# Output products of a graph layer, moved from the end of its edge loop into the loop

## The chip, the cores and the metric

The kernel runs on one core of a Trainium2 chip. The time is that of the device for one execution, in microseconds (us); the time before is the median of three executions. One more execution was taken by the hardware profiler, and all durations of single instructions come from that one.

In the profile, PE is the matrix engine (TensorE) and PEld its loading of weights, DVE the vector engine, ACT the scalar engine, POOL the GpSimd engine, SP the engine that issues most DMAs. L803 is line 803 of the kernel.

## The reference

Four graph layers follow one another over 1024 nodes with 512 features and 17408 edges. Each layer normalizes its input, applies a relu and adds its result to x. The edges are sorted by their receiving node `dst`.

```python
h = jnp.maximum(_layernorm(x, axis=-1), 0.0)
x = x + _L0_gnn_ref(h, edge_index, L0_gnn_weight, L0_gnn_bias)
h = jnp.maximum(_layernorm(x, axis=-1), 0.0)
x = x + _L1_gnn_ref(h, edge_attr_4, edge_attr_8, edge_index, ...)
h = jnp.maximum(_layernorm(x, axis=-1), 0.0)
x = x + _L2_gnn_ref(h, ...)
h = jnp.maximum(_layernorm(x, axis=-1), 0.0)
x = x + _L3_gnn_ref(h, src, dst, edge_type_8, edge_weight, ...)
```

The change touches the end of the second of them, L1 (block 1 in the kernel's numbering, which counts from 0):

```python
x0, x1 = _lin_irreps(x0, x1, W_up0, W_up1)
h = edge_feats
for W in (W_mlp1, W_mlp2, W_mlp3):
    h = SILU_2MOM * jax.nn.silu(h @ W / jnp.sqrt(jnp.float32(W.shape[0])))
tpw = h @ W_mlp4 / jnp.sqrt(jnp.float32(W_mlp4.shape[0]))
w1, w2, w3, w4 = jnp.split(tpw, 4, axis=-1)
s0 = x0[sender]
s1 = x1[sender]
p1 = w1 * s0 * y0
p2 = (w2 * s0)[:, :, None] * y1[:, None, :]
p3 = w3[:, :, None] * s1 * y0[:, None, :]
p4 = w4 * jnp.einsum('eum,em->eu', s1, y1) / SQRT3
m0 = jnp.concatenate([p1, p4], axis=-1)
m1 = jnp.concatenate([p2, p3], axis=1)
msg0 = jax.ops.segment_sum(m0, receiver, num_segments=num_nodes)
msg1 = jax.ops.segment_sum(m1, receiver, num_segments=num_nodes)
o0, o1 = _lin_irreps(msg0, msg1, W_out0, W_out1)
out = jnp.concatenate([o0, o1.reshape(num_nodes, 3 * MUL)], axis=-1)
return out / AVG_NUM_NEIGHBORS
```

So for every edge a message of 8 blocks of 128 features is made and summed at the edge's receiver; the sums of a node are then multiplied with two output matrices. These last two products, with the addition to x, are called the output products below. The layer after it, L2 (block 2), starts with the normalization and relu of the new x.

## The kernel before, in words

The nodes are cut into NB = 8 tiles of 128, the edges into NG = 68 groups of 256 (two tiles of 128 edges, G = 2). `stack(True)` is the arm of the kernel that runs for these inputs; in it a group's receivers lie in a window of W = 32 nodes, whose first node `base(g)` is read from memory into a register of DVE.

*Block 1's loop* (from line 870) runs over the groups. For group g it prepares the message of the next group and sums that of its own:

- `mixed(g + 1)`: four records on PE (L819, tile pw), the edge network's last product, from hidden values that SP loads (hq, L576).
- `message(g + 1)`: POOL gathers the senders' rows (L290, tile s), ACT makes six scaled copies (L836, dot), DVE five operations (L837 to L841) that write the message msg. The order of the operations on DVE, in the text, is: two products with pw, two additions of dot, one product with pw.
- `weighted(g + 1)`: POOL writes the receivers' one-hot rows, weighted (L859, yo).
- the sums of group g: 12 matmuls, 24 records on PE (L885, tile pg), into a bank of PSUM.
- `acc[:, :, base(g) : base(g) + W] += pg` on DVE (L888). acc holds the sums of all nodes, 8 blocks x 1024 nodes. Its place comes from a register, so nothing in the program says which nodes it touches.

From group 8 on, every fourth group also loads weights of block 2 or subtracts two of them on POOL (L765).

*Output products.* `out1(n)` multiplies node tile n of acc with the output matrices: 8 matmuls of 128 columns, 16 records on PE (L803, tile po), then two DVE operations that add the scaled result to x (L804, L806). At its end it calls `normed(n, "l2")`, the normalization and relu: DVE L208 and L209 (mean and variance), ACT L211 (root), DVE L217 and L219, ACT L227, which writes `h2[n]` (tile hl in the profile).

`settled(n)` is the number of the last group whose window can reach tile n: 11, 19, 28, 36, 45, 53, 62 for tiles 0 to 6. An input for which that doesn't hold takes the other arm. With EARLY = 2, `out1(0)` stands in the loop's group 66 and `out1(1)` in group 67. There the operations on DVE are kept in the written order by `pinned(DVE)`.

*After the loop*, `lagged(...)` (line 988) runs three stages over the tiles with a lag: `out1(n)` for the tiles not done yet, two tiles later the transposition of `h2` (`turned2`, PE L241, ACT L244), and one tile later still, for every second tile, the pair product `dense1` / `seven`: seven products of half size on PE (L955, 28 records) with DVE, ACT and POOL operations between them that end in the terms of block 2's propagation (L275).

*Order.* The program is written as one stream. A planner lays out each engine's queue at compile time: an instruction is put in the queue in the order of the text, unless it is not expected to be ready and a later one is. `pinned(...)` fixes the order of the instructions of an engine that are written in it, `issue_after(i)` puts instructions behind i on their engine. On the chip each engine works its queue in order and waits on semaphores.

*PSUM*: `bank(...)` gives one of four banks (pg, po, the transpositions, the pair products), `bank2(...)` one of two pairs of banks (pw). The normalized tiles `h` have four buffers, their small statistics two.

Of the kernel before, what the change touches and what calls it, by code (L numbers as in the profile page):

```python
# [23 lines left out]
NB = N // P  # L24
# [13 lines left out]
NG = ET // G  # L38
# [5 lines left out]
def settled(n):  # L44

    return (17 * (n + 1) + 1) // 2 + 2
# [3 lines left out]
def gnn_stack(ctx, tc, a, out, xtab, htabs, hidtab):  # L50
# [174 lines left out]
    def norm_relu(h, xn, name):  # L225
        rs, nm = stats(xn, name)
        rectified.append(nc.scalar.activation(h, xn, AF.Relu, bias=nm, scale=rs).ins)  # L227
# [4 lines left out]
    def normed(n, name):  # L232

        h = work.tile([P, D], F32, tag="h", name=f"h{name}_{n}", bufs=4)
        norm_relu(h, x[:, n, :], f"{name}_{n}")
        return h
# [26 lines left out]
    def lagged(*stages):  # L263

        for n in range(NB + max(lag for _, lag in stages)):
            for stage, lag in stages:
                if 0 <= n - lag < NB:
                    stage(n - lag)
# [118 lines left out]
    def stack(fast):  # L387
# [403 lines left out]
        EARLY = 2  # L791
        h2 = {}
# [3 lines left out]
        def out1(n):  # L796
            po = bank(f"po_{n}")
            ns = slice(n * P, (n + 1) * P)
            for c in range(KC):
                w = w_out0 if c == 0 else w_out1  # L800
                bl = (0, 1) if c == 0 else (1 + c, 4 + c)
                for k, b in enumerate(bl):
                    nc.tensor.matmul(po[:, c * P : (c + 1) * P], acc[:, b, ns], w[:, k, :], start=(k == 0), stop=(k == 1))  # L803
            nc.vector.scalar_tensor_tensor(x[:, n, :MUL], po[:, :MUL], scale, x[:, n, :MUL], op0=ALU.mult, op1=ALU.add)  # L804
            xm = x[:, n, MUL:].rearrange("p (u m) -> p m u", m=3)
            nc.vector.scalar_tensor_tensor(xm, po[:, MUL:].rearrange("p (m u) -> p m u", m=3), scale, xm, op0=ALU.mult, op1=ALU.add)  # L806
            h2[n] = normed(n, "l2")

        with tc.tile_pool(name=f"l1e{fast}", bufs=2 if fast else 1, reuse_waits="tile") as l1e:

            def mixed(g):

                q = g * G // 8
                if q not in hq:
                    fetch(q)
                pw = bank2(f"pw_{g}")
                for k in range(G):
                    t = g * G + k
                    nc.tensor.matmul(pw[:, k, :], hq[q][:, (t % 4) * P : (t % 4 + 1) * P], w_mlp4[:, t // 4 % 2, :],  # L819
                                     start=True, stop=True)  # L820
                return pw

            def message(g, pw):

                s = l1e.tile([P, G, D], F32, tag="s", name=f"s_{g}", bufs=3 if fast else 1)
                for k in range(G):
                    gather(s[:, k, :], xtab, src_i, g * G + k)
                w = pw.rearrange("p k (j u) -> p k j u", u=MUL)
                s0 = s[:, :, :MUL]
                s1 = s[:, :, MUL:].rearrange("p k (m u) -> p k m u", m=3)  # L830

                msg = l1e.tile([P, G, 6, MUL], F32, tag="msg", name=f"msg_{g}")
                dot = l1e.tile([P, G, 3, MUL], F32, tag="dot", name=f"dot_{g}", bufs=2 if fast else 1)
                for k in range(G):
                    for m in range(3):
                        nc.scalar.activation(dot[:, k, m, :], s1[:, k, m, :], AF.Copy, scale=ea[:, g * G + k, 1 + m : 2 + m])  # L836
                nc.vector.tensor_mul(msg[:, :, 0:2, :], w[:, :, 0:2, :], s0.unsqueeze(2).to_broadcast([P, G, 2, MUL]))  # L837
                nc.vector.tensor_mul(msg[:, :, 2:5, :], s1, w[:, :, 2:3, :].to_broadcast([P, G, 3, MUL]))  # L838
                nc.vector.tensor_add(dot[:, :, 0, :], dot[:, :, 0, :], dot[:, :, 1, :])
                nc.vector.tensor_add(dot[:, :, 0, :], dot[:, :, 0, :], dot[:, :, 2, :])  # L840
                nc.vector.tensor_mul(msg[:, :, 5, :], dot[:, :, 0, :], w[:, :, 3, :])  # L841
                return msg


            def blocks(msg, rhs):

                yield msg[:, 0, :], rhs(0, 1), 0, 1
                yield msg[:, 5, :], rhs(4, 1), 1, 1
                yield msg[:, 1, :], rhs(1, 3), 2, 3
                for m in range(3):  # L850
                    yield msg[:, 2 + m, :], rhs(0, 1), 5 + m, 1

            if fast:
                def weighted(g):
                    yo = l1e.tile([P, G, NY, W], F32, tag="yo", name=f"yo_{g}")
                    ts = slice(g * G, (g + 1) * G)
                    for k in range(G):
                        t = g * G + k
                        nc.gpsimd.tensor_mul(yo[:, k], ohw[:, t, :].unsqueeze(1).to_broadcast([P, NY, W]),  # L859
                                             ea[:, t, :].unsqueeze(2).to_broadcast([P, NY, W]))  # L860
                    return yo

                ahead = [weighted(0), weighted(1)]
                with pinned(PE, ACT):
                    fill(2)
                    pw = mixed(0)
                    fill(6)
                    nxt = message(0, pw), ahead.pop(0)
                    fill(3 * (NQ - NOW))
                for g in range(NG):  # L870
                    msg, yo = nxt
                    if g + 1 < NG:
                        nxt = message(g + 1, mixed(g + 1)), ahead.pop(0) if ahead else weighted(g + 1)
                    if g == 8:
                        blocks1 = load_l2()
                    if g >= 8 and g % 4 == 0:

                        with tc.issue_after(fetched[-1]):
                            next(blocks1, None)
                    ps = bank(f"pg_{g}")[:, : 8 * W].rearrange("p (b w) -> p b w", w=W)  # L880
                    prods = [list(blocks(msg[:, k], lambda y, n, k=k: yo[:, k, y : y + n, :])) for k in range(G)]
                    for i in range(len(prods[0])):
                        for k in range(G):
                            lhsT, rhs, b, n = prods[k][i]
                            nc.tensor.matmul(ps[:, b : b + n, :], lhsT, rhs, start=(k == 0), stop=(k == G - 1))  # L885
                    with pinned(DVE) if g >= NG - EARLY else nullcontext():
                        part = acc[:, :, bass.ds(base(g), W)]
                        nc.vector.tensor_add(part, part, ps)  # L888

                        if g >= NG - EARLY:  # L890
                            out1(g - NG + EARLY)
            else:
                for _ in load_l2():
                    pass
                for g in range(NG):
                    msg = message(g, mixed(g))
                    first = g == 0
                    for j in range(2):
                        for y, bl in ((0, ((0, 0), (2, 5), (3, 6), (4, 7))), (1, ((1, 2),)), (2, ((1, 3),)), (3, ((1, 4),)), (4, ((5, 1),))):
                            yo = l1e.tile([P, G, 512], F32, tag="yo", name=f"yo_{g}_{j}_{y}")  # L900
                            for k in range(G):
                                t = g * G + k
                                nc.vector.tensor_scalar(yo[:, k, :], iota[:, j * 512 : (j + 1) * 512], dst_f[:, t : t + 1],
                                                        ea[:, t, y : y + 1], op0=ALU.is_equal, op1=ALU.mult)
                            for c, b in bl:
                                ps = bank(f"pg_{g}_{j}_{b}")
                                for k in range(G):
                                    nc.tensor.matmul(ps, msg[:, k, c, :], yo[:, k, :], start=(k == 0), stop=(k == G - 1))
                                part = acc[:, b, j * 512 : (j + 1) * 512]
                                if first:  # L910
                                    nc.vector.tensor_copy(part, ps)
                                else:
                                    nc.vector.tensor_add(part, part, ps)
# [3 lines left out]
        with tc.tile_pool(name=f"l2{fast}", bufs=1) as l2:  # L917
# [67 lines left out]
                    for i in (n - 1, n):  # L985
                        nc.gpsimd.tensor_add(y[:, i, :], y[:, i, :], b1)

            lagged((lambda n: n in h2 or out1(n), 0), (turned2, 2), (dense1, 3))

            if fast:  # L990
                parts = l1.tile([P, 3, NB, D], BF16, tag="acc", name="parts2", bufs=1)
# [73 lines left out]
        with tc.tile_pool(name=f"l3{fast}", bufs=1, reuse_waits="tile") as l3:  # L1065
# [34 lines left out]
            for l in range(2):  # L1100
# [5 lines left out]
                with tc.tile_pool(name=f"l3e{l}{fast}", bufs=3 if fast else 1, reuse_waits="tile") as l3e:  # L1106
# [24 lines left out]
                    if fast:  # L1131
# [10 lines left out]
                        for g in range(NG):  # L1142
# [8 lines left out]
                            n = {0: 3, 1: 4, 2: 5, 4: 6, 6: 7}.get(g)  # L1151
# [109 lines left out]
```

## Time and profile before

| | |
|---|---|
| median of 3 executions | 1225.16 us (1224.23 to 1227.38) |
| profiled execution, its own time | 1221.29 us |
| its span, first to last instruction | 1219.5 us |
| mean granted clock of PE | 0.994 |
| PE busy in 340 to 380 us (inside the loop) | 40.00 of 40.00 us |
| DVE busy in 340 to 380 us | 28.78 of 40.00 us |
| ACT, POOL busy in 340 to 380 us | 17.87, 26.38 of 40.00 us |
| first pg of the loop, last pg | 178.6 us, 480.6 us |
| po of tile 0, po of tile 7 | 478.7 us, 523.3 us |
| one record of po in the trace, median | 275 ns (successive records overlap) |
| L804, L806 on DVE, median | 292 ns, 668 ns |
| first pair product of block 2 (L955) | 494.8 us |
| last pair product of block 2's first half ends, propagation starts | 551.0 us |
| granted clock below 1 | 108.7 to 112, 261.9 to 268.8, 483.9 to 487.3 us, and after the last matmul |

The engines run side by side; each works through its own queue. A line of the page with an arrow, "<-", names what an engine waited for before an instruction. A matmul's record in the trace lasts longer than its share of PE's time, since matmuls overlap; the chain of waits gives the share, as a stretch of several records.

### The profile page before, as it was taken

Reading aid. Unit: us, or ns where it says so; the run is one execution under the profiler, and the core shown is the slowest. Engines: PE = TensorE matmul, PEld = TensorE weight load, DVE = VectorE, ACT = ScalarE, POOL = GpSimd, SP = SyncE. Lnnn points to the kernel's source line nnn. Section 1 sums busy time; section 2 is a strip of 40 time slices with the busy share of each in tenths; the row PEclk is TensorE's granted clock in tenths of the full one; section 3 lists DMA queues with packets and bytes.
Section 4 is the critical chain, followed back from the end, with each engine's and each line's share of the span. In section 5 each row is a group of like instructions: output and inputs, shape, how many; then the busy total and the mean of one; then the engine's idle time right before and its main releaser. Section 6 shows DMA issues by size and latency. Waiting matters only on the chain.

```text
span 1219.5 us, 17420 instructions
## 1 busy us (share of the span) xinstructions
PE 1195.6 (98%) x6322; PEld 795.8 (65%) x6322; DVE 661.8 (54%) x1244; ACT 295.0 (24%) x693; POOL 580.5 (48%) x641
## 2 busy tenths in 40 slices
PE   7999999999999999999999999999999999999998
PEld 3445557767777778644444567777776577777774
DVE  5888647786777775776774433333332153333331
ACT  4435364434444443432332400000000000000000
POOL 2011346686666663443121266566661586555540
PEclk9999999989999999999999999999999999999999
DMA  3331045545544442002002366555552666556540
GB/s 114 124 125 36 22 155 165 151 139 153 151 139 139 139 130 85 21 22 65 1 9 92 101 193 206 160 164 157 165 163 65 199 170 194 162 162 170 157 129 17
DMA packets 55166, 149.77 MB, mean 123 GB/s; under 512 B 8796, under 2 KB 10272, under 8 KB 55008
## 3 DMA queue, kind: packets, MB, share of 16 engines
q0 software_dynamic: 33360, 109.34, 31.3%
q1 hardware_dynamic: 21424, 38.71, 9.6%
q8 instruction: 52, 0.85, 0.3%
q10 hardware_dynamic: 288, 0.52, 0.1%
q14 instruction: 42, 0.34, 0.1%
HBM read 135.70 MB, written 12.85 MB: 122 GB/s over the span
## 4 chain that ended last, share of the span: by engine, by line
PE 89%; DVE 4%; issue 2%; DMA 2%; ACT 1%; POOL 1%; DVEq 0%; SPq 0%; ACTq 0%; POOLq 0%
PE ps L1149 19%; PE po L1094 18%; PE pg L885 14%; PE pu L275 10%; PE pw L819 10%; PE p L955 7%; PE pl L251 4%; PE pm L453 2%; PE po L803 1%; PE pz L251 1%; PE pt_l L241 1%; PE pc L532 1%; DVE cnt L545 1%; PE pup L689 1%; DMA w_mlp<-in_L_gnn_W_mlp_dram 1%
## 5 line engine op out<-in xcount | busy, mean ns | idle before, releaser
L290 POOL DMA_INDIRECT m<-htab_dram,src_i x272 | 261.2, 960 | 165.6 <-PE ps L1149 116.9
L1149 PEld LDWEIGHTS ps<-wo,m 128*128 128x128 f32 x2176 | 261.6, 192 | 57.3 <-issue 56.0
L1149 PE MATMUL ps<-wo,m 128*128 128x128 f32 x2176 | 262.2, 275 | 0.7 <-DMA m<-htab_dram,src_i 0.7
L885 PEld LDWEIGHTS pg<-yo,msg 128*128 128x128 f32 x1632 | 194.6, 193 | 35.9 <-issue 17.8
L885 PE MATMUL pg<-yo,msg 128*128 128x32 f32 (+1 forms) x1632 | 189.8, 274 | 2.7 <-DVE msg L841 1.5
L1168 DVE TENSOR_TENSOR sums<-sums,ps 128x512 f32 x136 | 93.7, 689 | 156.7 <-PE po L1094 133.8
L836 ACT ACTIVATE dot<-s,ea 128x128 f32<-128x128 f32 x408 | 130.0, 390 | 165.7 <-DVE msg L841 107.5
L290 POOL DMA_INDIRECT s<-xtab_dram,src_i x136 | 132.8, 976 | 36.4 <-issue 24.5
L819 PE MATMUL pw<-w_mlp,hq 128*128 128x512 f32 x272 | 135.1, 620 | 0.0
L1135 DVE TENSOR_TENSOR wo<-ohw,cwTrue 128x256 f32<-128x256 f16 x136 | 65.9, 487 | 103.5 <-PE ps L1149 103.5
L859 POOL TENSOR_TENSOR yo<-ohw,ea 128x160 f32<-128x160 f16 x136 | 63.1, 486 | 66.6 <-PE pg L885 66.5
L275 PE MATMUL pu<-parts,cnt 128*128 128x512 bf16 x384 | 84.8, 379 | 0.0
L837 DVE TENSOR_TENSOR msg<-pw,s 128x512 f32<-128x512 f32 x68 | 47.0, 692 | 47.3 <-PE pw L819 35.6
L819 PEld LDWEIGHTS pw<-w_mlp,hq 128*128 128x128 f32 x272 | 47.2, 193 | 34.0 <-issue 34.0
L275 PEld LDWEIGHTS <-cnt 128*128 128x128 f16 x384 | 37.6, 98 | 44.9 <-issue 2.3
L838 DVE TENSOR_TENSOR msg<-s,pw 128x768 f32<-128x768 f32 x68 | 64.2, 944 | 0.0
L1094 PE MATMUL po<-basis_0True,sums 128*128 128x512 f32 x128 | 60.8, 600 | 0.4
L1094 PE MATMUL po<-basis_3True,sums 128*128 128x512 f32 x128 | 59.8, 594 | 0.8 <-DVE sums L1168 0.8
L1081 ACT ACTIVATE stage<-stage 128x512 f32<-128x512 f32 x8 | 5.0, 630 | 226.9 <-DVE stage L1080 226.9
L1094 PE MATMUL po<-w_l,sums 128*128 128x512 f32 x128 | 59.9, 593 | 0.0
L1094 PE MATMUL po<-basis_1True,sums 128*128 128x512 f32 x128 | 59.9, 593 | 0.0
L888 DVE TENSOR_TENSOR acc<-acc,pg 128x256 f32 x68 | 28.7, 422 | 46.7 <-PE pg L885 46.7
(208 smaller groups left out, 1355.2 us busy)
## 6 DMA issues: line engine op xcount, KB each, us to landing
hq<-hidtab_dram SPq DMA_DIRECT2D x17, 256.0 KB, 2.9
m<-htab_dram,src_i POOLq DMA_INDIRECT x272, 3.6
hidtab_dram<-hid POOLq DMA_DIRECT2D x9, 256.0 KB, 2.3
s<-xtab_dram,src_i POOLq DMA_INDIRECT x136, 3.6
xtab_dram<-up SPq DMA_DIRECT2D x8, 256.0 KB, 2.0
b_1True<-in_L_gnn_W_dram SPq DMA_DIRECT2D x4, 512.0 KB, 5.0
w_l<-in_L_gnn_basis_dram SPq DMA_DIRECT2D x4, 512.0 KB, 4.3
basis_0True<-in_L_gnn_basis_dram SPq DMA_DIRECT2D x4, 512.0 KB, 4.0
```

The costliest lines, as they stand in the source:

```text
L275: nc.tensor.matmul(pu, m[:, s, d * P : (d + 1) * P], z[:, s, :], start=(s == 0 and j == 0), stop=(s == NB - 1 and j == len(zs) - 1))
L290: nc.gpsimd.indirect_dma_start(out=g, out_offset=None, in_=table, in_offset=bass.IndirectOffsetOnAxis(ap=idx[:, t : t + 1], axis=0))
L819: nc.tensor.matmul(pw[:, k, :], hq[q][:, (t % 4) * P : (t % 4 + 1) * P], w_mlp4[:, t // 4 % 2, :], start=True, stop=True)
L836: nc.scalar.activation(dot[:, k, m, :], s1[:, k, m, :], AF.Copy, scale=ea[:, g * G + k, 1 + m : 2 + m])
L838: nc.vector.tensor_mul(msg[:, :, 2:5, :], s1, w[:, :, 2:3, :].to_broadcast([P, G, 3, MUL]))
L859: nc.gpsimd.tensor_mul(yo[:, k], ohw[:, t, :].unsqueeze(1).to_broadcast([P, NY, W]), ea[:, t, :].unsqueeze(2).to_broadcast([P, NY, W]))
L885: nc.tensor.matmul(ps[:, b : b + n, :], lhsT, rhs, start=(k == 0), stop=(k == G - 1))
L955: nc.tensor.matmul(p, lhs[:, c, :], rhs[:, c, :], start=(c == 0), stop=(c == 1))
L1094: nc.tensor.matmul(po, sums[:, c, b, n * P : (n + 1) * P], chunk(w3[1 + b], c), start=(b == 0 and c == 0), stop=(b == NBAS - 1 and c == KC ...
L1135: nc.vector.tensor_mul(wo, ohw[:, ts, :].unsqueeze(2).to_broadcast([P, G, NBAS, W]), cw[:, l, ts, :].unsqueeze(3).to_broadcast([P, G, NBAS ...
L1149: nc.tensor.matmul(ps[:, c * P : (c + 1) * P], m[k][:, c * P : (c + 1) * P], wo[:, k].rearrange("p b w -> p (b w)"), start=(k == 0), stop= ...
L1168: nc.vector.tensor_add(part, part, ps.rearrange("p (i w) -> p i w", w=W))
```

## The change

`out1(n)` is cut in two: the products and the addition to x keep the name, and the normalization becomes `norm1(n)`. In the loop, `out1(n)` for tiles 0 to 6 is called in group `settled(n) + 1`, that is in groups 12, 20, 29, 37, 46, 54 and 63, behind that group's addition into acc. Groups 66 and 67 call `norm1(0)` and `norm1(1)` where they called `out1(0)` and `out1(1)`. After the loop, the first stage of `lagged` calls `out1` for tile 7 alone, and `norm1` for the tiles that have no `h2` yet. In the arm that does not run here the calls are as before.

```diff
             nc.vector.scalar_tensor_tensor(xm, po[:, MUL:].rearrange("p (m u) -> p m u", m=3), scale, xm, op0=ALU.mult, op1=ALU.add)
+
+        def norm1(n):
             h2[n] = normed(n, "l2")
 
@@
                         part = acc[:, :, bass.ds(base(g), W)]
                         nc.vector.tensor_add(part, part, ps)
 
+                        for n in range(NB - 1):
+                            if g == settled(n) + 1:
+                                out1(n)
                         if g >= NG - EARLY:
-                            out1(g - NG + EARLY)
+                            norm1(g - NG + EARLY)
@@
-            lagged((lambda n: n in h2 or out1(n), 0), (turned2, 2), (dense1, 3))
+            def ended1(n):
+                if n == NB - 1 or not fast:
+                    out1(n)
+                if n not in h2:
+                    norm1(n)
+
+            lagged((ended1, 0), (turned2, 2), (dense1, 3))
```

## The prediction

> **What bounds the kernel now.** I read the page's busy table first, then the chain of waits from the end of block 1's loop on, then the windows, and at last the timeline of single engines around the places that the change touches.
>
> ```profile
> PE 1195.6 (98%) x6322; PEld 795.8 (65%) x6322; DVE 661.8 (54%) x1244; ACT 295.0 (24%) x693; POOL 580.5 (48%) x641
> ```
>
> PE is busy for 98% of the span of 1219.5 us, so 23.9 us is all that is not PE. A change that only moves PE work from one place to another is worth what it does to those gaps, and to the clock at which PE runs.
>
> The chain, in order of time (start us, us, what), at the end of the loop:
>
> ```profile
> 473.79 1.80 PE pw L819 x4
> 475.59 2.61 PE pg L885 x24
> 478.20 0.02 issue
> 478.22 0.43 DVE acc L888
> 478.65 0.04 issue
> 478.70 2.07 PE po L803 x16
> ...
> 484.15 5.31 PE po L803 x32
> ...
> 492.72 1.79 PE po L803 x16
> ...
> 494.94 12.02 PE p L955 x28
> ```
>
> One group of the loop costs PE 1.80 + 2.60 = 4.40 us, and one tile's output product 1.79 us. The product of tile 0 waits for the accumulation of the group just before it, though no window of that group reaches tile 0: the addition's place in acc comes from a register, so every product waits for the addition traced last before it. The first pair of block 2 begins at 494.94, after five of the eight products. The two products at 484.15 took 5.31 us for what costs 3.58 elsewhere. The windows say why (us, PE busy, granted clock, DMA share, GB/s; the second fence has all engines):
>
> ```profile
> 483.90:487.30 3.40, 3.15 (x15) 0.50 0.75 228
> ```
> ```profile
> 340.00:380.00 40.00, 40.00 (x257) 31.39 (x257) 28.78 (x56) 17.87 (x57) 26.38 (x37) 1.00 0.46 133
> ```
>
> For 3.4 us the clock stood at 0.50. Inside the loop it is 1.00, PE has no gap, and DVE works 28.78 of 40 us.
>
> PE's timeline at the loop's start:
>
> ```profile
> 178.60 0.97 PE L885 MATMUL pg<-yo,msg 128*128 128x32 f32 x8
> 179.89 2.42 PE L885 MATMUL pg<-yo,msg 128*128 128x32 f32 x20 [0.31 <-DVE msg L841]
> 182.14 1.96 PE L819 MATMUL pw<-w_mlp,hq 128*128 128x512 f32 x4
> ```
>
> A group has 24 records of pg. Here 28 stand ahead of the pw of group 2, so four of group 1 went before a pw that the code names first: PE's queue is laid out by what is expected to be ready, not by the text alone.
>
> **The change part by part.** Seven products (tiles 0 to 6) run in the loop at groups 12, 20, 29, 37, 46, 54 and 63; before, tiles 0 and 1 ran at groups 66 and 67, tiles 2 to 7 after the loop. Tile 7 stays. No DMA is issued by any moved step, so the queues of SP and POOL keep their contents.
>
> *PE work.* 7 x 1.79 = 12.5 us enters the loop, 5 x 1.79 leaves the stretch before the first pair, 2 x 1.79 (tiles 5 and 6) leaves the gaps between pairs. The sum is 0: the loop has no idle PE to take it in.
>
> *The wait for the addition, seven times.* At group 66 PE stood still for 0.51 us between pg and po (the timeline's idle figure). In the loop the next pw (1.80 us, its two banks free since the message two groups back was finished) needs nothing of that addition. If it goes first the price is 0; if the product keeps its written place, 7 x 0.51 = 3.6 us, and what is queued behind it is that pw, for which DVE's message product (L837) waits. I take 0, by the four records above, and keep 3.6 plus clock losses for the range.
>
> *The other engines.* Each product brings two DVE operations (0.29 + 0.67 = 0.96 us). DVE has 11.2 of 40 us free, that is 1.2 per group, and the group with a product lasts 6.19 us: 0. The cover is PE's own 4.40 us; without it 7 x 0.96 = 6.7 us would show. A bank of PSUM is held until L806 ends; there are four, and pg uses one or two. The next addition into acc must wait until the product has read it, but 2.6 us of pg lie between: 0.
>
> *What the loop's end gives up.* The waits before the products were 0.51 (tile 0) and 0.80 us (tile 1), another 0.38 stood before a transposition (waiting for hl), and the half clock cost 5.31 - 3.58 = 1.73. Together 3.4 us that can go.
>
> *What comes in its place.* DVE's timeline there:
>
> ```profile
> 478.22 0.42 DVE L888 TENSOR_TENSOR acc<-acc,pg 128x256 f32 x1 [0.71 <-PE pg L885]
> 478.56 0.42 DVE L840 TENSOR_TENSOR dot<-dot 128x256 f32<-128x256 f32 x1
> 479.01 0.42 DVE L841 TENSOR_TENSOR msg<-dot,pw 128x256 f32<-128x256 f32 x1
> 480.79 0.29 DVE L804 SCALAR_TENSOR_TENSOR x<-po,x 128x128 f32<-128x128 f32 x1 [1.35 <-PE po L803]
> 481.00 0.67 DVE L806 SCALAR_TENSOR_TENSOR x<-po,x 128x384 f32<-128x384 f32 x1
> 481.70 0.69 DVE L208 BATCH_NORM_STATS2 st_l<-x 128x6 f32<-128x512 f32 x1
> ```
>
> (a) The last group has no pw of a following group ahead of it; the product of tile 0 filled this hole. Its message is finished at 479.43, pg of group 66 at 478.20: PE now stands for 1.2 us. It is 0.2 if the two DVE operations go before L888, 1.9 if a normalization's 0.69 us comes between. I take 1.2, the order seen.
>
> (b) The clock. The 0.80 us wait, in a stretch with little but pg in it, was followed by 3.41 us of half clock; the 0.51 us wait, with a product behind it, by none. Two stretches of pg with 1.2 us between them are nearer to the first: I take one such stretch, 1.73. Bounds: 0, and the longer slow stretch inside the loop from 261.9 us on, after waits of 1.23 and 1.16 us, which cost 3.78 - 2.17 for 20 records of pg and 3.55 - 1.80 for a pw, 3.4 us.
>
> The Trainium skill, page "TensorE: Matmul & The Clock Gate", section "Part 1: The HAM clock gate (the "warmup" mystery)", has the clock fall to half after an idle window of about 3.4 us. The length of the slow stretch agrees with the row (3.41 us), the condition does not: here 0.80 us of idle was enough. By the rule (b) would be 0 and the sum below -0.8; by the row it is as taken.
>
> (c) The normalization of tile 1 is still pinned behind the last addition: 0.62 us for that (0.2 to start, 0.42), then from L208 at 481.70 to the end of hl at 484.23, 2.53 us, so 3.15 us from the end of pg. PE has a transposition (0.44) and the product of tile 7 (1.79) to put there, 2.2 us: 0.9 us of waiting, and 0.3 for tile 2, whose hl (0.81 us on ACT) follows that of tile 1 and hides half behind a transposition. I take 1.2. Lower bound 0: the rows of tiles 2 to 6 are final long before, so their normalizations may run in DVE's free 1.2 us per group. Upper bound 3.1, if tile 7's product keeps its place behind the pairs.
>
> (d) The pairs of block 2 now follow each other with only transpositions between them. Before, the pairs from 525.9 and 538.4 us stood like that, and PE waited 0.36 us for DVE's L949. Two more joints: between 0 and 0.7; I take 0.2, since each now has two transpositions (0.88 us) for cover.
>
> The sum: 0 + 0 - 3.4 + 1.2 + 1.7 + 1.2 + 0.2 = +0.9 us, on a span of 1219.5 (1221.29 with what lies around it). That execution lies 3.9 us below the median of the runs; I put the difference on the median: 1225.16 + 0.9 = 1226.1.
>
> **The rivals.**
>
> *Products stall the loop (slower).* Each product stands at the head of PE's queue until its addition is done. For it: so it was at groups 66 and 67. Against it: there no pw was left that could have gone first, and PE's order did bend at 182 us. Price: 7 x 0.51 = 3.6 us, plus the 0.9 above, and some half-clock stretches at 1.73 each; with two, +8.0: 1233.1, with none 1229.7. It decides when the mean wait per product is over 0.40 us (7 x 0.40 + 0.9 = 3.7).
>
> *The tail is bound by DVE and ACT (slower).* With five products gone from before the first pair, nothing covers the normalizations: (a) 1.9, (b) 3.4, (c) 3.1, (d) 0.7, less 3.4, is +5.7: 1230.9. For it: the chain already runs through five short DVE and ACT steps between 480.8 and 484; against it: DVE is busy 11.6 of the 16.4 us of a pair, and 1.9 of those leave.
>
> *A clean tail (faster).* The early normalizations run inside the loop, a transposition or a pair fills the hole before the last group, the clock stays up: (a) 0.2, (b) 0, (c) 0, (d) 0.2, less 3.4: -3.0, 1222.2. For it: additions of block 2's second bias to x (L1011) run at 484 us, as soon as x allows and some 65 us before their step in the code.
>
> *The loop's one bad spot moves (faster).* Between 252.9 and 268.7 us eight subtractions on POOL (L765) stand among the gathers, DVE's L839 takes 5.98 us beside them, and PE loses 1.23 + 1.16 + 3.4 = 5.8 us. An extra 1.79 us at group 12 shifts what meets there. If all of it goes: 1225.2 + 0.9 - 5.8 = 1220.3. Against it: loads, gathers and subtractions all follow PE's progress and should shift together.
>
> *It doesn't do what it says.* The queue could be laid out so that the products end up late again; then 1225.2. They are ahead of everything else in the text, so this is hardly worth a chance.
>
> **How the numbers follow.** Forecast (between -1.5 and +3.5 us) 0.40, stalled loop 0.24, bound tail 0.14, clean tail 0.13, moved spot 0.07, no effect 0.02. What a measurement here can tell from no change is about 0.3%, 3.7 us: below 1221.5 is faster, above 1228.8 slower. Faster: most of the moved spot (0.05), a third of the clean tail (0.04), a little of the forecast (0.03), 0.12. Slower: nine tenths of the stalled loop (0.22), three quarters of the bound tail (0.11), a little of the forecast (0.03), 0.36. The rest, 0.52, is same. The forecast's own range is 1223.7 to 1228.7. The range for 8 in 10 takes in the clean tail and the stalled loop with two slow stretches: 1221 to 1233.
>
> **What would show it.** Right: seven po groups of 16 records at about 235, 278, 320, 357, 398, 435 and 476 us (the end of pg of the group before the change, plus 1.79 for each product ahead and half a pw), each with a pw before it and no idle of PE; a wait of about 1.2 us before the last pg, one stretch of half clock behind it; the first pair at about 501 us (494.9 + 12.5 - 8.95 + 0.7 for the waits, and 1.8 for tile 7). Wrong: idle before po in the loop with acc named as the releaser, more than one half-clock stretch there, pg waiting for L841 in the groups after a product (DVE's two additions then were not free), or a slow stretch near 262 us of another length. A first pair later than 503 us without waits in the loop would say that (c) was too small.

## The result, and the profile after

| | before | after |
|---|---|---|
| median | 1223.65 us (1218.97 to 1227.38, 22 runs) | 1226.71 us (1224.35 to 1236.01, 22 runs) |
| ratio to before | | 1.0041, 95% interval 1.0027 to 1.0055 |
| profiled execution, its span | 1221.29, 1219.5 us | 1231.0, 1229.2 us |
| first pg of the loop to the start of block 2's propagation (pu) | 178.60 to 551.00: 372.4 us | 179.85 to 560.85: 381.0 us |
| end of pg of group 66 to pu | 478.20 to 551.00: 72.8 us | 496.09 to 560.85: 64.8 us |

Over all runs the change makes the kernel slower by 0.41%, some 5.0 us (3.3 to 6.7); the two medians lie 3.1 us apart. The profiled execution of the change is one of eight of the 22 that had a mean granted clock of 0.983 to 0.989 and took 1230.2 to 1236.0 us, while the other 14, at 0.992 or 0.993, took 1224.4 to 1227.1 us, so its trace must be read place by place and not by its span. The busy table says little, as before:

```profile
PE 1202.0 (98%) x6306; PEld 800.4 (65%) x6322; DVE 664.3 (54%) x1244; ACT 293.7 (24%) x693; POOL 578.2 (47%) x641
```

**The loop took the products for nothing.** PE's timeline around the product of tile 0 (start us, us, engine, line, operation, records, and in brackets idle time before it and its releaser):

```profile
235.31 1.96 PE L821 MATMUL pw<-w_mlp,hq 128*128 128x512 f32 x4
237.11 1.95 PE L803 MATMUL po<-w_out,acc 128*128 128x128 f32 x16
238.89 2.76 PE L887 MATMUL pg<-yo,msg 128*128 128x32 f32 x24
```

A pw stands between the group's pg and the product, and no bracket with idle time follows: while PE works on pw, DVE finishes the addition. The other six products look the same, at 284.8, 326.1 and so on to 482.7 us. From the bad spot of the loop on (to 281 us) to the end of pg of group 66 the stage grew by 10.71 us; six products are 6 x 1.79 = 10.74.

**The loss is at the loop's end.** The chain of waits from there on, in order of time (start us, us, what):

```profile
493.48 2.61 PE pg L887 x24
496.09 0.02 issue
...
496.45 0.42 DVE dot L842
496.87 0.60 DVE st_l L208
497.48 0.33 DVE msg L843
...
497.85 3.70 PE pg L887 x20
501.55 0.02 issue
501.57 0.42 DVE acc L890
502.00 1.20 DVE st_l L208 x2
...
504.60 0.82 ACT hl L227
505.43 0.04 issue
505.47 1.97 PE pt_c L241 x8
```

From 496.09 to 497.85 it runs through DVE: the last message waits behind an addition of dot and behind the statistics (L208) of tile 0's normalization. From 501.55 to 505.47 it runs through the normalization of tile 1. PE had for these 3.9 us one transposition (pt_c), that of tile 0. PE's timeline has these holes as idle time:

```profile
497.85 3.69 PE L887 MATMUL pg<-yo,msg 128*128 128x32 f32 x20 [1.33 <-DVE msg L843]
...
505.47 1.97 PE L241 MATMUL pt_c<-ident,hl 128*128 128x128 f32 x8 [3.03 <-ACT hl L227]
```

Before, the chain left PE twice as well: from 480.76 to 484.15 us it ran through the additions of tile 0 to x, tile 0's normalization and the last addition into acc, and from 489.92 to 492.07 us through a copy and the rest of tile 1's normalization, both on ACT and DVE. But then PE had ready work beside it, the last pg and the product of tile 3, and stood idle for 0.80 and 0.38 us only. PE's timeline before:

```profile
480.59 2.76 PE L885 MATMUL pg<-yo,msg 128*128 128x32 f32 x24
484.15 5.31 PE L803 MATMUL po<-w_out,acc 128*128 128x128 f32 x32 [0.80 <-DVE acc L888]
...
489.74 1.95 PE L803 MATMUL po<-w_out,acc 128*128 128x128 f32 x16
492.07 0.65 PE L241 MATMUL pt_c<-ident,hl 128*128 128x128 f32 x4 [0.38 <-ACT hl L227]
```

Between and behind the two holes PE ran at half clock (us, busy time and instructions of PE, PEld, DVE, ACT, POOL, then the granted clock, the DMA share and GB/s):

```profile
492.00:498.70 6.70, 5.37 (x39) 4.51 (x38) 4.51 (x12) 0.30 (x2) 0.70 (x2) 1.00 0.01 2
498.70:508.94 10.24, 7.21 (x30) 5.72 (x30) 6.35 (x21) 5.83 (x11) 4.44 (x4) 0.50 0.44 154
508.94:515.00 6.06, 6.06 (x16) 2.71 (x15) 4.87 (x11) 3.41 (x8) 3.14 (x4) 1.00 0.01 1
```

The 20 records of pg took 3.70 us instead of 2.17, and the two transpositions 1.76 (505.47 to 507.23, where the first pair begins) instead of 0.88; that of tile 0, inside the second hole, took 0.89 instead of 0.44.

The account: from the end of pg of group 66 to pu the stage lost 72.80 - 64.76 = 8.04 us, while 7 x 1.79 = 12.53 us of products left it. So 4.5 us were lost here.

**The bad spot** of the loop, which the change does not touch, cost this execution another 4.5 us. Its two waits are those of before, the half clock behind them lasted 17.07 us (from 263.2) instead of 6.83:

```profile
262.25 0.60 PE L887 MATMUL pg<-yo,msg 128*128 128x32 f32 x4 [1.22 <-DVE msg L839]
264.02 4.48 PE L887 MATMUL pg<-yo,msg 128*128 128x32 f32 x20 [1.16 <-DVE msg L843]
```

Whether that belongs to the change is tested below.

### The profile page after: what moved, and what is told of

Same layout as the page of the kernel before. It is cut to its first block, busy times and chain, and to the rows that moved or that the text cites. A ratio compares the mean times of both kernels' runs of the same rounds, so it can differ in the third digit from the quotient of the medians.

```text
span 1229.2 us, 17393 instructions
## 1 busy us (share of the span) xinstructions
PE 1202.0 (98%) x6306; PEld 800.4 (65%) x6322; DVE 664.3 (54%) x1244; ACT 293.7 (24%) x693; POOL 578.2 (47%) x641
## 4 chain that ended last, share of the span: by engine, by line
PE 90%; DVE 3%; issue 2%; DMA 2%; ACT 1%; POOL 1%; DVEq 0%; SPq 0%; ACTq 0%; POOLq 0%
PE ps L1160 19%; PE po L1105 18%; PE pg L887 15%; PE pu L275 10%; PE pw L821 10%; PE p L960 7%; PE pl L251 4%; PE pm L453 2%; PE po L803 1%; PE pz L251 1%; PE pt_l L241 1%; PE pc L532 1%; PE pup L689 1%; DVE cnt L545 1%; PE pt_c L241 1%
## 5 line engine op out<-in xcount | busy, mean ns | idle before, releaser
L887 PEld LDWEIGHTS pg<-yo,msg 128*128 128x128 f32 x1632 | 198.3, 197 | 34.0 <-issue 16.6
L887 PE MATMUL pg<-yo,msg 128*128 128x32 f32 (+1 forms) x1632 | 194.0, 277 | 3.7 <-DVE msg L843 2.5
```

## The experiments

The theory, **"end"**: inside the loop the products are free; the seven products were the work that covered two chains of short DVE and ACT operations (the last message, the normalization of tile 1), and without them PE waits and loses its clock. The rivals: **"spot"** (the change makes the bad spot of the loop worse) and **"loop"** (each product in the loop costs a little that no single wait shows).

All kernels of the table do the same work between the first pg and pu, in another order (the one with idle products adds 8 records), so the length of that stretch in the profiled execution can be compared directly; it is one execution of each, with the half clock that this one had. Waits are PE's, as the timeline puts them down to another engine, without a first one of 0.3 to 0.8 us near 180 us, which every kernel but the change has; "half clock" is the length of the stretches, in us, in the loop and from 465 us on.

| kernel | ratio to before, interval | pg to pu | waits, loop / end | half clock, loop / end |
|---|---|---|---|---|
| before | 1 | 372.4 | 2.4 / 2.1 | 6.8 / 3.4 |
| the change | 1.0041 (1.0027 to 1.0055) | 381.0 | 2.4 / 4.7 | 17.1 / 10.2 |
| change, normalizations in the loop | 1.0053 (1.0033 to 1.0074) | 373.8 | 4.5 / 0.6 | 10.2 / 0 |
| change, idle products | 1.0059 (1.0034 to 1.0085) | 378.0 | 2.4 / 4.3 | 6.8 / 0 |
| before, spaced | 0.9948 (0.9928 to 0.9969) | 365.1 | 0 / 2.0 | 0 / 0 |
| change, spaced | 0.9987 (0.9969 to 1.0005) | 373.1 | 0 / 4.7 | 0 / 13.7 |
| spaced, tiles 0 and 1 left at the end | 1.0023 (1.0008 to 1.0038) | 374.4 | 0 / 6.5 | 0 / 10.2 |
| spaced, tile 7 first | 0.9998 (0.9981 to 1.0014) | 372.4 | 0 / 5.4 | 0 / 6.8 |
| spaced, three late as cover | 0.9961 (0.9947 to 0.9975) | 367.1 | 0 / 3.4 | 0 / 0 |
| three late as cover, not spaced | 0.9993 (0.9970 to 1.0016) | 375.5 | 2.4 / 3.4 | 13.7 / 0 |
| spaced, three late, normalizations earlier | 0.9970 (0.9949 to 0.9991) | 368.8 | 0 / 3.4 | 0 / 3.4 |
| before, spaced, again | 0.9952 (0.9933 to 0.9972) | 368.3 | 0 / 1.8 | 0 / 6.8 |

The last two ran on another chip than the other experiments, on which before took 1232.37 us; they compare with each other.

### Normalizations in the loop

```diff
                             if g == settled(n) + 1:
                                 out1(n)
-                        if g >= NG - EARLY:
-                            norm1(g - NG + EARLY)
+                            if n < 4 and g == settled(n) + 2:
+                                norm1(n)
```

> The change, and besides the normalizations of tiles 0 to 3 called in the loop, each one group after its product. Theory 'end' (what the change costs is PE standing at the loop's end, 3.0 us for the normalization of tile 1 and 1.3 us before the last pg, and the half clock behind these waits): the 3.0 us wait is gone, at most one stretch of half clock is left, the time from the end of the last-but-one pg to the first pair falls from 11.4 us to 4 to 7, and the ratio to the kernel before is 0.997 to 1.000. Rival 'spot' (the cost is the longer half clock near 262 us, and the end is no worse than before): the ratio stays at about 1.004.

Measured: 1.0053, so the expected gain did not come, and the interval holds the 1.004 that "spot" expected: the time alone speaks for "spot" here. In the profile the theory held at the end: the waits of 1.33 and 3.03 us are gone, one of 0.24 is left, the clock stays up, and the first pair follows without a hole. But the same DVE operations now delay messages inside the loop. PE's timeline of this kernel:

```profile
248.42 2.84 PE L887 MATMUL pg<-yo,msg 128*128 128x32 f32 x24 [0.51 <-DVE nm_l L219]
255.27 3.10 PE L887 MATMUL pg<-yo,msg 128*128 128x32 f32 x17 [2.21 <-DVE msg L843]
```

The timeline puts the first wait down to a step of the normalization itself, which stands among the message's operations on DVE; at 318.9, 340.5 and 378.3 us come 0.78, 0.38 and 0.64 more. (The 2.21 us are the bad spot: DVE's L841 takes 4.59 us just before, beside POOL's L765.) The waits in the loop grew by 2.1 us and those at the end shrank by 4.1, so its profile alone would make it faster than the change. Its nine runs, 1223.04 to 1235.17 us, do not show that. The profiled one was the fastest of them and had the highest mean granted clock, 0.994, while the others had 0.985 to 0.993; so most of what the others lost goes with the clock, but at which place stays open.

### Idle products in the holes

```diff
                         if g >= NG - EARLY:
                             norm1(g - NG + EARLY)
+                            with tc.issue_after(summing):
+                                idle = bank(f"idle_{g}")
+                                for i in range((1, 3)[g - NG + EARLY]):
+                                    nc.tensor.matmul(idle, ident, w_mlp4[:, 0, :], start=True, stop=True)
```

> The change, and besides products that nothing reads (w_mlp4 with the identity, 0.9 us each): one behind the pg of group 66, three behind that of group 67. The waits stay as long, only PE is not idle in them. If the half clock at the loop's end comes from PE's idle time, the clock stays at 1.00 from 490 us on, pg of the last group takes 2.6 us and not 4.3, the transpositions 0.44 and not 1.0, and the kernel is 3 to 4 us faster than the change: ratio 1.000 to 1.002. If the waits alone are the cost, the ratio stays at 1.004; if the added products stand in the way, 1.005 to 1.007. Rival 'spot': no change from 1.004.

Measured: 1.0059, slower than before and no better than the change, as was expected if the added products stand in the way (1.0034 to 1.0085 does not exclude 1.004). In the profiled execution, with the added products, which nobody reads, the clock stayed at 1.00 from the loop's end on. That agrees with PE's idle time as the cause of the half clock; it does not prove it, since a wait of 2.69 us was left there and no half clock followed. The time did not get better. PE's timeline, and then ACT's:

```profile
491.84 2.42 PE L887 MATMUL pg<-yo,msg 128*128 128x32 f32 x20 [0.47 <-DVE msg L843]
494.10 2.82 PE L900 MATMUL idle<-w_mlp,ident 128*128 128x512 f32 x6
496.76 0.60 PE L241 MATMUL pt_c<-ident,hl 128*128 128x128 f32 x4
500.04 1.43 PE L241 MATMUL pt_c<-ident,hl 128*128 128x128 f32 x8 [2.69 <-ACT hl L227]
```
```profile
497.39 0.59 ACT L244 COPY hT_c<-pt_c 128x512 f32<-128x512 f32 x1 [3.89 <-PE pt_c L241]
497.88 0.30 ACT L211 ACTIVATE sd_l<-mv_l,eps 128x1 f32<-128x1 f32 x1
```

The idle products stand ahead of the transposition of tile 0. Its copy on ACT waits for it and stands ahead of the root of tile 1 (L211) in ACT's queue, and the next transposition waits for that root. Tile 1's mean and variance were done at 495.99 us, its root began at 497.88. Cover that delays the head of the chain is no cover.

### The bad spot taken out of both

POOL's eight subtractions of weights (L765) ran in a burst among the gathers; each is now queued behind the one-hot rows of its own group (`wrote` holds POOL's instructions that write them), in the kernel before and in the change:

```diff
-                        with tc.issue_after(fetched[-1]):
+                        with tc.issue_after(fetched[-1]), tc.issue_after(wrote[-1]):
                             next(blocks1, None)
```

Before, spaced:

> The kernel before, with each subtraction of block 2's weights on POOL queued behind the one-hot rows of the group in which it is written (groups 28 to 56, every fourth), in place of all eight near 250 to 265 us. If the slow spot near 262 us comes from POOL's subtractions standing among the gathers, the two waits (1.2 us each) and the 6.8 us of half clock are gone: 5 to 6 us less, ratio 0.995 to 0.996. If the spot has another cause, 1.000.

The change, spaced:

> The change, with the subtractions spaced in the same way. Theory 'end': it stays 4 to 5 us slower than the kernel before with the spacing: ratio to the kernel before 0.999 to 1.000. Rival 'spot' (the change's cost lies in the spot): it is as fast as the kernel before with the spacing, ratio 0.995 to 0.996.

Measured: 0.9948 and 0.9987. In both, the waits and the half clock of the loop are gone; what is left between them is the end. PE's timeline there, first of spaced before, then of the spaced change:

```profile
470.79 2.05 PE L803 MATMUL po<-w_out,acc 128*128 128x128 f32 x16 [0.51 <-DVE acc L889]
...
476.24 3.84 PE L803 MATMUL po<-w_out,acc 128*128 128x128 f32 x32 [0.80 <-DVE acc L889]
...
482.68 0.66 PE L241 MATMUL pt_c<-ident,hl 128*128 128x128 f32 x4 [0.38 <-ACT hl L227]
```
```profile
487.58 4.45 PE L888 MATMUL pg<-yo,msg 128*128 128x32 f32 x20 [1.33 <-DVE msg L843]
491.84 1.09 PE L241 MATMUL pt_c<-ident,hl 128*128 128x128 f32 x4
495.96 1.97 PE L241 MATMUL pt_c<-ident,hl 128*128 128x128 f32 x8 [3.02 <-ACT hl L227]
```

The difference of the ratios, 0.39%, is near that of the kernels with the spot (0.41%), so "spot" falls as the whole cause: the change costs about as much without it. The two intervals allow some 0.1 to 0.7%, so a part of the cost at the spot is not excluded.

The clocks of these runs say how the loss divides (an estimate). Over the 34 executions of before on this chip, 0.001 of mean granted clock went with 1.1 us. Spaced before had a mean clock of 0.9973 over its six executions, the spaced change 0.9939 over its twelve: some 3.9 of the 6.0 us between their means (1214.9 and 1221.0 us). The other 2.1 us are near the 2.7 by which the waits grew in the profiles.

### Two products left, five in the loop

```diff
-                            if g == settled(n) + 1:
+                            if n >= EARLY and g == settled(n) + 1:
                                 out1(n)
                         if g >= NG - EARLY:
+                            out1(g - NG + EARLY)
                             norm1(g - NG + EARLY)
```

> The change, with POOL's subtractions spaced out as in the spaced pair, and only five products (tiles 2 to 6) in the loop: tiles 0 and 1 keep product and normalization at groups 66 and 67, as before. Theory 'end' (the loop takes products for nothing, and the loss is the two holes that the missing products leave after pg of groups 66 and 67, with their half clock): two products are cover enough for the first hole and for most of the second, so 0.994 to 0.996 of before, as spaced before (0.9948). Theory 'loop' (each product in the loop costs some 0.7 us that no single wait shows): five sevenths of the loss stay, 0.997 to 0.998.

Measured: 1.0023, worse than all seven in the loop (0.9987), and a miss for both theories. "Loop" is refuted: from the first pg to the last it took 305.32 us, spaced before took 296.19, and 296.19 + 5 x 1.79 is 305.14, so the products cost there what they cost elsewhere. "End" was right on the place and wrong on what covers what:

```profile
487.62 3.42 PE L803 MATMUL po<-w_out,acc 128*128 128x128 f32 x16 [0.80 <-DVE acc L891]
490.88 0.60 PE L241 MATMUL pt_c<-ident,hl 128*128 128x128 f32 x4
495.55 1.97 PE L241 MATMUL pt_c<-ident,hl 128*128 128x128 f32 x8 [4.07 <-ACT hl L227]
```

A product of tile 1 at the end covers nothing for tile 1. It is part of the chain: its normalization can only begin when it has been added to x. What covered that chain before were the products of tiles 2 and 3, which stood behind it (in spaced before 0.38 us of it were left bare), and this kernel, like the change, has them in the loop.

### Tile 7's product first

Tile 7's product, which the change leaves behind the first pairs, goes directly behind the last addition:

```diff
                         if g >= NG - EARLY:
                             norm1(g - NG + EARLY)
+                            if g == NG - 1:
+                                out1(NB - 1)
@@
-                if n == NB - 1 or not fast:
+                if not fast:
                     out1(n)
```

> The change, spaced, with tile 7's product put directly behind the last addition instead of behind the first pairs. Theory 'end, (c)': the wait of 3.02 us before the transposition of tile 1 shrinks by about 1.8 us to 1.2; the hole of 1.33 us before the last pg and half clock behind it stay; so 1.8 to 3.5 us less than the spaced change (0.9987): 0.996 to 0.9975. Rival 'chain': the product's two DVE operations go ahead of tile 1's normalization and lengthen it, so that the wait stays and the time is that of the spaced change, 0.998 to 0.9995.

Measured: 0.9998; against the spaced change (0.9987) the intervals overlap, and the expected gain of 1.8 to 3.5 us is not there. The hole of 1.33 us before the last pg stayed. The wait before tile 1's transposition shrank as expected, and others took its place:

```profile
491.68 3.38 PE L803 MATMUL po<-w_out,acc 128*128 128x128 f32 x16 [0.51 <-DVE acc L891]
...
496.88 0.66 PE L241 MATMUL pt_c<-ident,hl 128*128 128x128 f32 x4 [1.39 <-ACT hl L227]
497.77 0.66 PE L241 MATMUL pt_c<-ident,hl 128*128 128x128 f32 x4 [0.23 <-ACT hl L227]
```

0.51 + 1.39 + 0.23, and 0.47 and 1.12 inside the first pair, where DVE is late: 3.72 us against 3.02. The rival "chain" is nearer.

### Three late products as cover

Products of tiles 0 to 4 in the loop; 5 at group 66, 6 and 7 at group 67, each behind the normalization that it is to cover. Once spaced, once not:

```diff
-                            if g == settled(n) + 1:
+                            if n < 5 and g == settled(n) + 1:
                                 out1(n)
                         if g >= NG - EARLY:
                             norm1(g - NG + EARLY)
+                            out1(5 + g - NG + EARLY)
+                        if g == NG - 1:
+                            out1(NB - 1)
@@
-                if n == NB - 1 or not fast:
+                if not fast:
                     out1(n)
```

> The change, spaced, with five products (tiles 0 to 4) in the loop and the three late tiles as cover at its end: tile 0's normalization and then tile 5's product at group 66, tile 1's normalization and then the products of tiles 6 and 7 at group 67. Theory 'end': PE has 1.79 us for the hole of 1.33 and 3.58 for the one of 3.02, neither product waits for work that stands behind it, and the clock stays full: the waits that spaced before still had at this place (0.51, 0.80, 0.38) go as well, so 0.993 to 0.995 of before, level with spaced before or up to 1.7 us under it. Theory 'loop': five products in the loop keep five sevenths of the loss, 0.997 to 0.998.

> The same without the spacing, so against before only the products' places differ: five in the loop, three at the end as cover. Theory 'end': 0.998 to 1.000 (1.3 to 1.7 us of waits less at the end; the bad spot of the loop stays, whatever it costs in that execution). Theory 'loop': 1.002 to 1.004, near the change's 1.0041.

Measured: 0.9961 and 0.9993. The second is as "end" expected; the first lies between the two expectations, just above the 0.993 to 0.995 of "end" and below the 0.997 to 0.998 of "loop", and its interval reaches into both; "loop" had fallen with the kernel above. PE's timeline of the spaced one:

```profile
482.48 2.05 PE L803 MATMUL po<-w_out,acc 128*128 128x128 f32 x16 [0.51 <-DVE acc L891]
...
487.64 3.84 PE L803 MATMUL po<-w_out,acc 128*128 128x128 f32 x32 [0.51 <-DVE acc L891]
491.32 1.04 PE L241 MATMUL pt_c<-ident,hl 128*128 128x128 f32 x8
493.79 0.66 PE L241 MATMUL pt_c<-ident,hl 128*128 128x128 f32 x4 [1.44 <-ACT hl L227]
```

With work behind the start of each chain the 1.33 and 3.02 us are gone, and in this execution the half clock too: some 3.2 us (0.26%) come back against the spaced change, with five products still in the loop (the two intervals just meet, at 0.9969 to 0.9975). What is late next is the transposition of tile 2 (1.44).

### Normalizations earlier still, beside spaced before

Products of tiles 5 and 6 ahead of the addition of group 66, that of tile 7 behind the transposition of tile 1, normalizations of tiles 0, 1 and 2 at groups 65, 66 and 67:

```diff
+                        if g == NG - 2:
+                            out1(NB - 3)
+                            out1(NB - 2)
                         part = acc[:, :, bass.ds(base(g), W)]
                         nc.vector.tensor_add(part, part, ps)
 
-                        for n in range(NB - 1):
+                        for n in range(NB - 3):
                             if g == settled(n) + 1:
                                 out1(n)
-                        if g >= NG - EARLY:
-                            norm1(g - NG + EARLY)
+                        if g >= NG - 3:
+                            norm1(g - NG + 3)
@@
                 hT2[n] = transposed(h2[n], f"c1_{n}")
+                if fast and n == 1:
+                    out1(NB - 1)
@@
-                if n == NB - 1 or not fast:
+                if not fast:
                     out1(n)
```

> Spaced, products of tiles 0 to 4 in the loop; those of tiles 5 and 6 at group 66 ahead of its addition (they wait for no fresh addition), that of tile 7 behind the transposition of tile 1; the normalizations of tiles 0, 1 and 2 one group earlier each, at groups 65, 66 and 67. Theory 'end': nothing at the end waits for what was just begun, so the 0.51, 0.51, 1.44 and 0.60 us of the three-late version go, and no half clock comes: 2 to 3 us under it, 0.993 to 0.995 of before, and 0.2 to 2 us under spaced before. Rival 'nothing to gain' (PE is the bound and spaced before has only some 2 us of waits left there; what the earlier normalizations take from DVE delays messages again, as the earlier run of normalizations in the loop showed): 0.995 to 0.997, level with or slower than spaced before.

> Spaced before once more, on the same chip and beside the run above, so that the two can be set against each other: 0.9948 again (0.993 to 0.997).

Measured: 0.9970, and spaced before again 0.9952, as the rival "nothing to gain" had it. A wait of 2.16 us was left before the transposition of tile 1; ACT's timeline shows whose it is:

```profile
490.47 0.59 ACT L244 COPY hT_c<-pt_c 128x512 f32<-128x512 f32 x1 [11.79 <-PE pt_c L241]
490.95 0.30 ACT L211 ACTIVATE sd_l<-mv_l,eps 128x1 f32<-128x1 f32 x1
```

Tile 1's mean and variance were done at 489.43 us, but its root stands behind the copy of tile 0's transposition in ACT's queue, as with the idle products. Of the kernels tried, none with moved products is faster than spaced before, in which all products stay where they were. That one beats both kernels of this case: 0.9948 (0.9928 to 0.9969), median 1214.97 us of six executions.

## Why the prediction was right and wrong

The time put down, 1226.1 us, lies beside the median of 1226.71, and most of the chance (0.88) stood on no measurable difference or on slower. That is luck in part, and better than the reasoning deserves: the sum said +0.9 us, measured is +5.0 (3.3 to 6.7), outside the forecast's own -1.5 to +3.5. The base helped: the three runs of before had their median at 1225.16, the 22 runs now have 1223.65, from which the same sum gives 1224.6.

- *The wait for the addition*, taken 0: right. Each of the seven products has a pw before it and no idle. With it the likeliest rival, "Products stall the loop" (0.24), fell. The four records at 182 us were the right evidence.
- *PE work* and *the other engines*, 0: right. Six products cost 10.71 us in the loop, 10.74 predicted.
- *What the loop's end gives up*, 3.4: right in kind; the waits of 0.51, 0.80 and 0.38 us of before are gone.
- *(a) The hole before the last pg*, 1.2: PE was idle for 1.33 us. The order on DVE was that of the upper case, 1.76 us from pg to pg with the statistics (L208) between L842 and L843, but four records of the last pg went ahead into the hole and took 0.43 of it.
- *(b) The clock*, one stretch, 1.73: **a size that failed**, by 2.0 us. It was 10.24 us long, three times the stretch of before, from 498.70 us, just behind (a), over (c) and into the first pair; it slowed pg (+1.53), three transpositions (+1.3) and the first 1.71 us of the first pair (+0.85), 3.7 us, above the upper bound of 3.4. Other executions of the change may have had another length.
- *(c) The normalization of tile 1*, 1.2: **the step that failed**, by 1.8 us. It was 3.03 us, near the upper bound of 3.1. The product of tile 7, which was to fill 1.79 us of it, kept its place behind the first pairs (533 us). And the chain has three statistics, 1.20 and 0.58 us, where one of 0.69 was reckoned: those of two more tiles stood among tile 1's operations on DVE.
- *(d)*, 0.2: 0; the one wait of 0.35 us (L954) was there before as 0.36 (L949).

With the measured sizes the same sum is 0 - 3.4 + 1.3 + 3.7 + 3.0 + 0 = +4.6, against 4.5 in that stage. So what happened was nearest to the rival "The tail is bound by DVE and ACT" (1230.9, +5.7), which had 0.14. Its evidence was on the page, the chain of five short DVE and ACT steps; the argument against it looked at how busy DVE is during a pair, which has nothing to do with the length of one chain at the loop's end. "A clean tail" needed the normalizations to move by themselves; they did not. "The loop's one bad spot moves" fell: the spot shifted by some 3 us with the same two waits. But half clock of another length behind it (17.07 us) was among the prediction's own signs of being wrong, and it came in the profiled execution; and of POOL's eight subtractions, which the prediction placed between 252.9 and 268.7 us, the first began at 248.97. The first pair began at 507.23 us, later than the 503 that was to speak against (c), but 4.5 us of that are the spot's, so that sign decides nothing.

The Trainium skill, page "TensorE: Matmul & The Clock Gate", section "Part 1: The HAM clock gate (the "warmup" mystery)", speaks of a free-running window of about 3.4 us. The lengths agree: 3.41, 6.83, 10.24, 13.65 and 17.07 us in these runs, whole multiples. Its condition of an idle window does not: in the change's loop waits of 1.22 and 1.16 us stood ahead of 17.07 us of half clock, as the prediction chose to believe from the row of 0.80 us.

## What to carry to other kernels

Before work is moved off a stage's end into a loop that can take it, look at what stands beside it there: on an engine that is busy all the time, work at a joint can be the cover of the chains of short operations that cross the joint, and it is then worth the part of those chains that nothing else covers. What counts as cover is ready work that stands *behind* the start of the chain and not in it; ask for each piece that is taken away which chain was running meanwhile, and lay the steps of that chain end to end. In such a chain look at each engine's queue too: a copy that waits for PE and stands ahead of a root on ACT makes the two take turns.

## What the runs showed of the hardware

Two additions on DVE with both inputs and the output in SBUF took 5.96 and 3.12 us where they take 0.42 elsewhere, while POOL worked on the subtractions; DVE's timeline of the change:

```profile
255.55 5.96 DVE L841 TENSOR_TENSOR dot<-dot 128x256 f32<-128x256 f32 x1
...
265.35 3.12 DVE L841 TENSOR_TENSOR dot<-dot 128x256 f32<-128x256 f32 x1
```

POOL's timeline beside the first:

```profile
255.48 1.28 POOL L765 TENSOR_TENSOR t_1True<-b_1True 128x512 f32<-128x512 f32 x1
256.70 2.49 POOL L765 TENSOR_TENSOR b_1True<-b_1True 128x512 f32<-128x512 f32 x2
259.15 0.86 POOL L861 TENSOR_TENSOR yo<-ohw,ea 128x160 f32<-128x160 f16 x2
259.97 1.25 POOL L765 TENSOR_TENSOR t_1True<-b_1True 128x512 f32<-128x512 f32 x1
```

Spreading eight such POOL instructions over the loop was worth 0.5% of the whole kernel, more than anything that was done to the products. The Trainium skill, page "SBUF — State Buffer", section "Who interferes with whom", has a DVE instruction with two SBUF inputs and a GpSimd instruction that reads SBUF exclude each other, and the rows agree in kind: the first addition ended with the last of four subtractions of some 1.25 us each and the one-hot rows between them.

The half clock did not follow the waits alone. Spaced before showed none at its end in one execution and 6.83 us in another, on another chip, with waits of 0.51 and 0.80 in the one and 0.51 and 0.57 in the other; three late products, spaced, had a wait of 1.44 us and none, the idle products one of 2.69 us and none; the bad spot had waits of 1.2 and 1.2 us and between 3.41 and 17.07 us of half clock. The cause of that spread was not tried.
